# One stream of parts for all images, six product buffers, and delta*x made a third of the channels at a time

## The chip, the cores and the metric

The kernel runs on one core of one Trainium2 chip. Time is device microseconds of one execution of the whole program; of the kernel before, three runs are given and their median is used. One more execution was recorded by the profiler, and every duration below comes from it.

Five engines work side by side, each on its own queue of instructions in program order: PE (matrix products; PEld is its weight load), DVE (vector), ACT (scalar functions), POOL (a second vector engine) and SP, which here only issues DMAs. They wait for one another through semaphores.

## The reference

Eight images of 56 x 56 positions and 192 channels pass through four layers. Each adds to x a function of its group-normalised input:

```python
x = x + gated_toeplitz(_gn(x))      # layer 0: silu(p) * (toeplitz along w + along h of q*v), projected
x = x + window_attention(_gn(x))    # layer 1: 7x7 windows, shifted by 3, 6 heads
x = x + depthwise_conv3x3(_gn(x))   # layer 2
x = x + selective_scan_2d(_gn(x))   # layer 3
```

Layer 3 is most of the work. From 384 inner channels u (after a projection, a 3x3 depthwise convolution and silu) it runs four scans over the 3136 positions: by rows, by columns, and both backwards. Each channel has 16 states:

```python
delta = softplus(delta + delta_bias)
dA  = exp(delta * A)                       # per channel, state and position
dBu = delta * u * Bm
h[l] = dA[l] * h[l-1] + dBu[l]             # the scan
y[l] = sum over states of h[l] * Cm[l]  +  D * u[l]
```

The four y are added, layer-normalised over the channels, multiplied by silu(z), projected to 192 channels and added to x. All of it is float32.

## The kernel before, in words

Three stages come first, for all images: the products q*v, the Toeplitz products of layer 0, and constants. Then, per image, there are three kinds of work.

**The front** of an image, `front(b)`, is a Python generator over five parts: `gate` (rest of layer 0), `attention` (layer 1), `conv2` (layer 2), `inner` (projection, convolution and silu of layer 3, three times 128 channels) and `steps`. `steps` runs over 14 groups (o, j): two orders o of the positions (rows, columns) and seven chunks j of 448 positions. A group makes B and C (one product into a bank, L851; a copy, L853; stored to `bc_d`) and delta for the two scans of that order (products at L861, ACT at L866, Softplus at L870), and stores delta to `dl_d`. All parts of all fronts use the same memory, `slab`, one part at a time. Front 0 runs alone, before any scan.

**The scans** of an image run over 4 slots (the four directions) x 7 chunks of 448 positions x 3 thirds d of the channels x 8 pairs k of states: `chunks` lists (image, slot, chunk) for all images, 224 in all, and `pairs` lists (chunk i, d, k), 5376 in all. For each pair g:

- `inject` (L991, POOL): hs = du * bm, where du = delta * x of this third (`times_x`, L979, POOL) and bm is B, sent to all partitions. hs has 5 buffers; it is issued two pairs ahead, by `feed`.
- `decay` (L1006, ACT): dA = exp(delta * A), two instructions into one of two PSUM buffers `ps_a`, one pair ahead.
- `scan` (L1015, DVE), then `times_c` (L1021): hc = h * cm, on POOL for k in (1, 4, 6), otherwise on DVE. hc has 4 buffers. POOL's product is issued one pair later than the scan.
- `add_up` (L1036, PE): the product of hc with an identity adds the states up in a PSUM bank; it is issued two pairs after the scan and frees hc. After eight pairs `sums` adds the bank to `ysum` on DVE (L1046 in slot 0, with D * x; L1050 otherwise).

The loads for the scans are all issued on SP: bm and cm of the next chunk by `load_bc`, a pair at a time in the last third; delta of the next chunk by `load_delta` and three thirds of x by `load_xc` (tile xcd, 4 buffers) at d = 1, k = 0. The three products `times_x` for the next chunk stand at (d, k) = (1, 6), (1, 7) and (2, 0); du has 4 buffers. In slot 0 another load of x, for `sums`, is issued at k = 2 and used at k = 4.

**The finish** of an image, `finish(b, j)`, normalises and projects chunk j of `ysum` (L883 to L935); it runs beside the first seven chunks of the next image's scans, each of which overwrites `ysum` again.

The order of instructions is fixed while the program is built. A class `Parts` holds generators (clients), and a model of when each engine is free (`t`, with prices in us such as 1.1 for a pair's `add_up`). After each pair the loop calls `parts.step(limit)`: for each client it issues the next bit of work as long as the model says that it fits under a limit for ACT, PE ("E") and DVE. A client that has a PSUM bank holds it until its next turn. Where work has to be complete, the loop calls `step(anything)`, with no limit, until it is:

```python
if i % (4 * NCH) == 0 and d == 0 and k == 0 and b + 1 < B:
    fronts[b + 1] = parts.add(front(b + 1), "front")
...
if i + 1 in range(4 * NCH, len(chunks), 4 * NCH):
    while fronts[b + 1] in parts.clients:
        parts.step(anything)
```

So front b + 1 begins with the scans of image b and must be complete in the last chunk of image b, at d = 1, k = 0 (L1173 to L1175). The last image has no front beside it.

Of the kernel before, what the change touches and what calls it, by code (L numbers as in the profile page):

```python
# [15 lines left out]
F32 = mybir.dt.float32  # L16
# [11 lines left out]
CH = 448  # L28
NCH = L // CH
# [4 lines left out]
ND = DI // 128  # L34
NG = 2
# [46 lines left out]
def model(ctx: ExitStack, tc: tile.TileContext, a: dict, out: bass.AP):  # L82
    nc = tc.nc
    B = out.shape[0]
# [195 lines left out]
    with (  # L280
# [79 lines left out]


        meter, costs = Meter(tc.nc), {}


        st = wp.tile([CP, 2, NCH, 6], F32, name="gn_st")
# [466 lines left out]
        def steps(b):  # L832

            w_x, xc, rc, dl = carve(slab, 128, (2, ND, 128), (2, ND, CH), (2, CH), (2, ND, CH))
            nc.sync.dma_start(out=w_x, in_=a["w_x"])
            todo = [(o, j) for o in range(2) for j in range(NCH)]

            def load_x(n):
                o, j = todo[n]
                nc.sync.dma_start(out=xc[:, n % 2], in_=xc_d[o][b][:, :, j * CH : (j + 1) * CH])  # L840

            load_x(0)
            yield 0, 0, 8.0
            for n, (o, j) in enumerate(todo):
                tok = slice(j * CH, (j + 1) * CH)
                if n + 1 < len(todo):
                    load_x(n + 1)
                yield 0, 1
                p = bank()
                for d in range(ND):  # L850
                    nc.tensor.matmul(p[:, :CH], w_x[:, o, d, :], xc[:, n % 2, d, :], start=d == 0, stop=d == ND - 1)  # L851
                yield 1, 0
                nc.scalar.copy(rc[:, n % 2, :], p[:, :CH])  # L853
                nc.sync.dma_start(out=bc_d[o][b][:, tok], in_=rc[64:, n % 2, :])
                for d in range(ND):
                    yield 0, 2
                    held = []
                    for s in range(2):
                        row = slice(32 * s, 32 * s + R)
                        held.append(bank())  # L860
                        nc.tensor.matmul(  # L861
                            held[s][:, :CH], w_dt[row, o, d * 128 : (d + 1) * 128], rc[row, n % 2, :], start=True, stop=True
                        )
                    yield 2, 0
                    for s in range(2):
                        nc.scalar.activation(  # L866
                            dl[:, s, d, :], held[s][:, :CH], AF.Identity, bias=dt_b[:, 2 * o + s, d : d + 1]
                        )
                yield 0, 0
                nc.scalar.activation(dl, dl, AF.Softplus)  # L870
                usual_functions()
                for s in range(2):
                    nc.sync.dma_start(out=dl_d[2 * o + s][b][:, :, tok], in_=dl[:, s])
            yield 0, 0

        def front(b):
            yield from gate(b)
            yield from attention(b)
            yield from conv2(b)
            yield from inner(b)  # L880
            yield from steps(b)
# [83 lines left out]

        def load_xc(i, d):
            b, slot, j = chunks[i]
            t = sp.tile([128, CH], F32, name="xcd", bufs=4)
            nc.sync.dma_start(out=t, in_=xc_d[slot // 2][b][:, d, j * CH : (j + 1) * CH])
            return t  # L970

# [3 lines left out]
            nc.sync.dma_start(out=delta[:, :, 1 : CH + 1], in_=dl_d[slot][b][:, :, j * CH : (j + 1) * CH])  # L975

        def times_x(i, d):
            du = dus[i, d] = sp.tile([128, 1, CH], F32, name="du", bufs=4)
            nc.gpsimd.tensor_mul(du[:, 0, :], deltas[i][:, d, 1 : CH + 1], xcs.pop((i, d)))  # L979

        def tokens(i):
# [35 lines left out]
        def times_c(g):  # L1017
            i, d, k = pairs[g]
            h = hss[g] if on_pool(d, k) else das[g]
            hc = hcs[g] = sp.tile([128, NG, CH], F32, name="hc", bufs=4)  # L1020
            (nc.gpsimd if on_pool(d, k) else nc.vector).tensor_mul(hc, h[:, :, tokens(i)[0]], cms[i, k])  # L1021

        def keep_state(g):
# [29 lines left out]
        class Parts:  # L1053
# [8 lines left out]
            def run(self, engine, cost, *after):  # L1062
                self.t[engine] = max(self.t[engine], 0.0, *after) + cost
                return self.t[engine]
# [25 lines left out]
                entry.held, entry.needs, *load = got  # L1090
                entry.ready = at + sum(load)

            def step(self, limit):
                old = [e for e in self.clients if e.held]
                for entry in old + [e for e in self.clients if e not in old]:
                    while entry in self.clients:
                        if entry.held and entry not in old:
                            break
                        if entry.needs + sum(e.held for e in self.clients if e is not entry) > 2:
                            break  # L1100
                        if not self.fits(entry, limit):
                            entry.waits += 1
                            break
                        entry.waits = 0
                        if entry in old:
                            old.remove(entry)
                        self.resume(entry)
# [27 lines left out]
        with tc.manual_schedule():  # L1135
            for k in range(NP):
                load_bc(0, k)
            load_delta(0)
            for d in range(ND):
                xcs[0, d] = load_xc(0, d)  # L1140
                times_x(0, d)
            ahead, last = 2, len(pairs) - 1
            parts = Parts()
            run = parts.run
# [6 lines left out]

            def take(g):
                times_c(g)
                after = scanned[g], summed[g - 4] if g > 3 else 0.0
                taken[g] = run("P", 2.0, *after) if on_pool(*pairs[g][1:]) else run("D", 1.09, *after)

            def prepare(g):
# [4 lines left out]
                feed(g)  # L1162
            initial(0), initial(1)
            prepare(0)
            fronts = {}
            ending, anything = None, dict.fromkeys("ADE", 1e9)
            for g, (i, d, k) in enumerate(pairs):
                b, slot, j = chunks[i]
                if i % (4 * NCH) == 0 and d == 0 and k == 0 and b + 1 < B:
                    fronts[b + 1] = parts.add(front(b + 1), "front")  # L1170
                more = i + 1 < len(chunks)
                if more and d == 1 and k == 0:
                    if i + 1 in range(4 * NCH, len(chunks), 4 * NCH):  # L1173
                        while fronts[b + 1] in parts.clients:
                            parts.step(anything)  # L1175
                    load_delta(i + 1)
                    for e in range(ND):
                        xcs[i + 1, e] = load_xc(i + 1, e)
                if more and (d, k) in ((1, 6), (1, 7), (2, 0)):
                    times_x(i + 1, d + k - 7 if d == 1 else 2)  # L1180
                    run("P", 1.08)
                pi, pd, pk = pairs[g - 1]
                if g + ahead <= last:
                    feed(g + ahead)
                if g and on_pool(pd, pk):
                    take(g - 1)
                if g:
                    keep_state(g - 1)
                    run("A", 0.15, scanned[g - 1])
                if g < last:  # L1190
                    prepare(g + 1)
                if g + 2 <= last:
                    initial(g + 2)
                    run("A", 0.12, taken[g - 3] if g > 2 else 0.0)
                scan(g)
                scanned[g] = run("D", 2.02, set_[g], fed[g])
                if not on_pool(d, k):
                    take(g)
                if g and pd == ND - 1 and pi + 1 < len(chunks):
                    load_bc(pi + 1, pk)  # L1200
                done = (i, d - 1) if d else (i - 1, ND - 1)
                if k == 2 and g > NP and chunks[done[0]][1] == 0:
                    xds[done] = load_xc(*done)
                if slot == 0 and b > 0 and (d, k) == (1, 4):
                    while ending.at < 3:
                        parts.step(anything)
                if k == 4 and g > NP:
                    sums(*done)
                if slot == 0 and b > 0 and ((j, d, k) == (0, 0, 5) or j + 1 < NCH and (d, k) == (2, 4)):
                    while ending in parts.clients:  # L1210
                        parts.step(anything)
                    ending = parts.add(finish(b - 1, j + (d == 2)), "finish")

                n1 = max(parts.t["D"], fed[g + 1], set_[g + 1])
                n2 = n1 + (2.02 if on_pool(*pairs[min(g + 1, last)][1:]) else 3.11)
                parts.step({"A": max(n2, fed[g + 2]) - 0.7, "E": n1 + 5.0, "D": 0.2})
                if g >= 2:
                    add_up(g - 2)
                    summed[g - 2] = run("E", 1.1, taken[g - 2])
# [108 lines left out]
```

## Time and profile before

| | |
|---|---|
| three runs, us | 23,043.6, 23,055.5 (median), 23,061.3 |
| profiled execution: its own time, its span | 23,085.3, 23,083.3 |
| first scan; last product of `add_up` | 3,727; 22,879 |
| PE, DVE, ACT, POOL busy in the span | 80%, 72%, 54%, 70% |
| mean granted PE clock | 0.887 |
| time of one image's scans, images 0 to 7 | 2331, 2486, 2469, 2468, 2453, 2467, 2459, 2014 |

The span is from the first to the last instruction that the profiler saw. Busy PE time is modelled and overlaps, so a PE share of 80% is not a share of its peak. The image times run from an image's first scan to that of the next image. In the views of the profile, "x" is a count, and a row of waits names who waited, for whom, the time in total, how often, and the longest. A wait for several semaphores is put down to the one that came last.

### The profile page before, as it was taken

Reading aid. Unit: us, or ns where it says so; the run is one execution under the profiler, and the core shown is the slowest. Engines: PE = TensorE matmul, PEld = TensorE weight load, DVE = VectorE, ACT = ScalarE, POOL = GpSimd, SP = SyncE. Lnnn points to the kernel's source line nnn. Section 1 sums busy time; section 2 is a strip of 40 time slices with the busy share of each in tenths; the row PEclk is TensorE's granted clock in tenths of the full one; section 3 lists DMA queues with packets and bytes.
Section 4 is the critical chain, followed back from the end, with each engine's and each line's share of the span. In section 5 each row is a group of like instructions: output and inputs, shape, how many; then the busy total and the mean of one; then the engine's idle time right before and its main releaser. Section 6 shows DMA issues by size and latency. Waiting matters only on the chain. (4 is left out here: it accounts for less than half of the span.)

```text
span 23083.3 us, 201064 instructions
## 1 busy us (share of the span) xinstructions
PE 18554.5 (80%) x58660; PEld 9730.9 (42%) x58660; DVE 16579.4 (72%) x13156; ACT 12534.0 (54%) x31864; POOL 16157.3 (70%) x8500
## 2 busy tenths in 40 slices
PE   8866678888887878888888888887888798887666
PEld 4566334434443435343543444343434353333323
DVE  3211114997789768986899778976898689877996
ACT  3211225655666565756565566656664657565554
POOL 0000004987789768976898778877897689778997
PEclk9987778999899989998999889998999899988888
DMA  3488225445544455345544454345534553454332
GB/s 89 109 196 178 67 62 171 135 123 168 167 135 131 142 169 146 124 135 172 151 134 129 161 162 137 122 147 177 148 115 146 168 157 119 140 172 139 126 122 89
DMA packets 2536339, 3220.44 MB, mean 140 GB/s; under 512 B 1045261, under 2 KB 2488687, under 8 KB 2504272
## 3 DMA queue, kind: packets, MB, share of 16 engines
q1 hardware_dynamic: 2515010, 3091.32, 45.2%
q0 software_dynamic: 15520, 116.14, 1.3%
q8 instruction: 465, 7.62, 0.1%
q14 instruction: 640, 5.24, 0.1%
q10 hardware_dynamic: 4704, 0.12, 0.0%
HBM read 2631.56 MB, written 575.48 MB: 139 GB/s over the span
## 5 line engine op out<-in xcount | busy, mean ns | idle before, releaser
L991 POOL TENSOR_TENSOR hs<-du,bm 128x896 f32<-128x896 f32 x5376 | 11124.4, 2102 | 110.1 <-DVE ps_a L1015 90.2
L1036 PE MATMUL ps_y<-hc,ident_sb 128*128 128x448 f32 x21504 | 9913.8, 597 | 947.8 <-POOL hc L1021 846.4
L1015 DVE TENSOR_TENSOR_SCAN ps_a<-ps_a,hs 128x898 f32<-128x898 f32 x3360 | 6793.9, 2022 | 1048.5 <-ACT ps_a L1006 871.5
L1006 ACT ACTIVATE ps_a<-delta,A_logs_sb 128x449 f32<-128x449 f32 x10752 | 6859.4, 638 | 322.2 <-DVE hs L1015 35.9
L1036 PEld LDWEIGHTS ps_y<-hc,ident_sb 128*128 128x128 f32 x21504 | 4339.0, 210 | 5095.4 <-issue 3594.3
L1021 POOL TENSOR_TENSOR hc<-hs,cm 128x896 f32<-128x896 f32 x2016 | 4067.0, 2017 | 2757.2 <-DVE hs L1015 1574.0
L1015 DVE TENSOR_TENSOR_SCAN hs<-ps_a,hs 128x898 f32<-128x898 f32 x2016 | 4064.5, 2016 | 810.3 <-ACT ps_a L1006 779.3
L1021 DVE TENSOR_TENSOR hc<-ps_a,cm 128x896 f32<-128x896 f32 x3360 | 3668.9, 1092 | 1166.1 <-PE ps_y L1036 883.2
L1028 ACT COPY state<-ps_a 128x2 f32<-128x2 f32 x3359 | 528.6, 157 | 4109.0 <-DVE hc L1021 4106.4
L979 POOL TENSOR_TENSOR du<-delta,xcd 128x448 f32<-128x448 f32 x672 | 716.0, 1066 | 1266.1 <-DMA xcd<-xc 1266.1
L263 PE MATMUL ps_tz<-tzx,tm 112*112 112x112 f32 x4608 | 889.3, 369 | 463.5 <-issue 294.7
L802 PE MATMUL ps_f<-slab 128*128 128x448 f32 x2646 | 1096.9, 551 | 85.0 <-DMA slab<-dg_d 58.0
L277 POOL DMA_DIRECT2D o<-tzx x192 | 97.8, 513 | 1490.9 <-DVE tzx L269 1340.1
L263 PEld LDWEIGHTS ps_tz<-tzx,tm 112*112 112x112 f32 x4608 | 883.8, 199 | 469.2 <-issue 468.1
L269 DVE COPY tzx<-ps_tz 112x448 f32<-112x448 f32 x288 | 179.9, 625 | 1172.3 <-PE ps_tz L263 862.0
L996 ACT COPY hs<-state 128x2 f32<-128x2 f32 x4608 | 817.5, 177 | 2.7 <-POOL hc L1021 2.6
L76 PE MATMUL ps_f<-slab 96*96 96x448 f32 (+6 forms) x2306 | 745.3, 519 | 76.1 <-DMA slab<-x 37.4
L269 ACT COPY tzx<-ps_tz 112x448 f32<-112x448 f32 x288 | 153.2, 532 | 1198.1 <-PE ps_tz L263 1067.2
L632 PE MATMUL ps_f<-ident_sb,slab 98*98 98x98 f32 x1344 | 337.9, 322 | 576.3 <-ACT slab L625 576.3
L734 PE MATMUL ps_f<-slab 96*96 96x448 f32 x1764 | 728.9, 549 | 46.4 <-DVE slab L721 46.4
L802 PEld LDWEIGHTS ps_f<-slab 128*128 128x128 f32 x2646 | 509.4, 193 | 598.0 <-issue 528.7
L861 PE MATMUL ps_f<-slab,w_dt_sb 12*128 12x448 f32 x1176 | 507.5, 787 | 309.8 <-ACT slab L853 234.9
(215 smaller groups left out, 17788.8 us busy)
## 6 DMA issues: line engine op xcount, KB each, us to landing
bm<-bc SPq DMA_DIRECT2D x1792, 448.0 KB
cm<-bc SPq DMA_DIRECT2D x1792, 448.0 KB
xcd<-xc SPq DMA_DIRECT2D x840, 224.0 KB
dl<-slab SPq DMA_DIRECT2D x224, 672.0 KB
delta<-dl SPq DMA_DIRECT2D x224, 672.0 KB
tzx<-qv SPq DMA_DIRECT2D x192, 588.0 KB
o<-tzx POOLq DMA_DIRECT2D x192, 588.0 KB, 16.3
slab<-x SPq DMA_DIRECT2D x224, 336.0 KB
```

The lines of the kernel that those rows point to most:

```text
L76: return f(*args, **kw)
L263: nc.tensor.matmul(po[:, c, :], t[:, c2 + c, :], x[:, :, c1 + c2 + c], start=True, stop=True)
L734: nc.tensor.matmul(p[:CP, :CH], dg[:, k, t, :], xp[:, u, k, dy : dy + 8, dx : dx + W], start=t == 0, stop=t == 8,)
L802: nc.tensor.matmul(p[:, :CH], dg[:, t, :], xp[:, 8 * j + dy : 8 * j + dy + 8, dx : dx + W], start=t == 0, stop=t == 8,)
L979: nc.gpsimd.tensor_mul(du[:, 0, :], deltas[i][:, d, 1 : CH + 1], xcs.pop((i, d)))
L991: nc.gpsimd.tensor_mul(hs[:, :, tokens(i)[0]], dus[i, d].to_broadcast([128, NG, CH]), bms[i, k])
L996: nc.scalar.copy(hss[g][:, :, tokens(i)[1]], src)
L1006: nc.scalar.activation(dA[:, n, :], deltas[i][:, d, at : at + CH + 1], AF.Exp, scale=negA[:, slot, d, c : c + 1])
L1015: nc.vector.tensor_tensor_scan(h, dA, hs, 0.0, ALU.mult, ALU.add)
L1021: (nc.gpsimd if on_pool(d, k) else nc.vector).tensor_mul(hc, h[:, :, tokens(i)[0]], cms[i, k])
L1028: nc.scalar.copy(states[i][:, d, NG * k : NG * k + NG], h[:, :, tokens(i)[2]])
L1036: nc.tensor.matmul(yps[i, d][:, :CH], ident, hcs[g][:, n, :], start=k + n == 0, stop=k + n == NP + NG - 2)
```

## The change

Three things are done together.

1. **One stream of fronts.** A new front is added whenever the one before is complete, not at the first pair of an image. A set `made` records which (image, o, j) groups of `steps` have been issued. Before `load_delta(i + 1)` the loop asks only that the group that chunk i + 1 reads is in it. `step` gets an argument `only`: where a front or a finish is forced, the other client goes on only if it holds a bank.
2. **Buffers.** hc has 6 buffers instead of 4, and the model knows it (`summed[g - 6]`). xcd and du have 2 instead of 4, which is the same memory. The limit for PE is 8.0 us after the next scan's start instead of 5.0.
3. **x and delta * x by thirds.** x of the next third is loaded at k = 0 of each third and multiplied with delta at k = 3 (in the last third, for the first third of the next chunk). The total of both stays the same.

```diff
+        made = set()
...
                 for s in range(2):
                     nc.sync.dma_start(out=dl_d[2 * o + s][b][:, :, tok], in_=dl[:, s])
+                made.add((b, o, j))
...
-            t = sp.tile([128, CH], F32, name="xcd", bufs=4)
+            t = sp.tile([128, CH], F32, name="xcd", bufs=2)
...
-            du = dus[i, d] = sp.tile([128, 1, CH], F32, name="du", bufs=4)
+            du = dus[i, d] = sp.tile([128, 1, CH], F32, name="du", bufs=2)
...
-            hc = hcs[g] = sp.tile([128, NG, CH], F32, name="hc", bufs=4)
+            hc = hcs[g] = sp.tile([128, NG, CH], F32, name="hc", bufs=6)
...
-            def step(self, limit):
+            def step(self, limit, only=None):
                 old = [e for e in self.clients if e.held]
                 for entry in old + [e for e in self.clients if e not in old]:
+                    if only is not None and entry is not only and not entry.held:
+                        continue
...
-            for d in range(ND):
-                xcs[0, d] = load_xc(0, d)
-                times_x(0, d)
+            xcs[0, 0] = load_xc(0, 0)
+            times_x(0, 0)
...
-                after = scanned[g], summed[g - 4] if g > 3 else 0.0
+                after = scanned[g], summed[g - 6] if g > 5 else 0.0
...
-            fronts = {}
+            ahead_of, b_next = None, 1
...
-                if i % (4 * NCH) == 0 and d == 0 and k == 0 and b + 1 < B:
-                    fronts[b + 1] = parts.add(front(b + 1), "front")
+                if ahead_of not in parts.clients and b_next < B:
+                    ahead_of = parts.add(front(b_next), "front")
+                    b_next += 1
                 more = i + 1 < len(chunks)
                 if more and d == 1 and k == 0:
-                    if i + 1 in range(4 * NCH, len(chunks), 4 * NCH):
-                        while fronts[b + 1] in parts.clients:
-                            parts.step(anything)
+                    b1, slot1, j1 = chunks[i + 1]
+                    while (b1, slot1 // 2, j1) not in made:
+                        parts.step(anything, ahead_of)
                     load_delta(i + 1)
-                    for e in range(ND):
-                        xcs[i + 1, e] = load_xc(i + 1, e)
-                if more and (d, k) in ((1, 6), (1, 7), (2, 0)):
-                    times_x(i + 1, d + k - 7 if d == 1 else 2)
-                    run("P", 1.08)
+                if k in (0, 3) and (d + 1 < ND or more):
+                    at = (i, d + 1) if d + 1 < ND else (i + 1, 0)
+                    if k == 0:
+                        xcs[at] = load_xc(*at)
+                    else:
+                        times_x(*at)
+                        run("P", 1.08)
...
                     while ending.at < 3:
-                        parts.step(anything)
+                        parts.step(anything, ending)
...
                     while ending in parts.clients:
-                        parts.step(anything)
+                        parts.step(anything, ending)
...
-                parts.step({"A": max(n2, fed[g + 2]) - 0.7, "E": n1 + 5.0, "D": 0.2})
+                parts.step({"A": max(n2, fed[g + 2]) - 0.7, "E": n1 + 8.0, "D": 0.2})
```

## The prediction

> **What bounds the kernel now.** I read first the page's busy shares: no engine is above 80%, so no single engine sets the 23,083 us; the answer must differ by stage. So I cut the trace at the first scan of a chunk (a chunk is 24 pairs) and asked the view of busy time by windows for one middle image and for the last one. The columns are: stretch, length, then PE, PEld, DVE, ACT, POOL busy, granted clock, DMA share, GB/s.
>
> ```profile
> 11118.00:11660.00 542.00, 479.49 (x1828) 274.65 (x1826) 448.20 (x354) 318.27 (x775) 453.15 (x240) 0.95 0.54 150
> 11660.00:12421.00 761.00, 613.14 (x2133) 298.30 (x2132) 715.19 (x607) 527.62 (x1656) 704.70 (x362) 0.91 0.41 126
> 12611.00:13159.00 548.00, 458.46 (x1168) 227.27 (x1166) 404.55 (x267) 301.21 (x685) 419.15 (x216) 0.91 0.48 154
> 13159.00:13329.00 170.00, 140.80 (x332) 57.99 (x332) 131.72 (x84) 134.62 (x267) 142.41 (x74) 0.84 0.59 205
> 13329.00:13481.00 152.00, 114.84 (x213) 45.36 (x211) 65.67 (x43) 96.50 (x161) 65.32 (x34) 0.72 0.43 145
> ...
> 21415.00:22809.00 1394.00, 937.64 (x1921) 418.78 (x1920) 1306.39 (x841) 733.44 (x1920) 1394.00 (x719) 0.87 0.38 125
> ```
>
> The last row is the floor: 20 chunks of image 7 with no other work beside them, 1394/20 = 69.7 us a chunk, POOL busy all the time. The others are image 3: chunks 1 to 6 (gate and finish) 90.3 us each, 7 to 15 and most of 16 (attention) about 76, 19 to 24 (inner) 91.3, 25 and 26 (steps) 85.0. **Then one chunk, the last, takes 152 us**, in which POOL and DVE are busy only 65 and 66 us. The view of waits for that stretch, "engine line <- what it waited for: us, times, longest", tells why; beside it are the waits of chunks 19 to 24, and two rows of the whole run:
>
> ```profile
> POOL hc L1021 <- DVE hs L1015: 79.6, 1, 79.6
> DVE hs L1015 <- ACT ps_a L1006: 75.1, 1, 75.1
> ```
> ```profile
> ACT slab L811 <- PE ps_f L802: 84.1, 21, 5.2
> ...
> DVE hc L1021 <- PE ps_y L1036: 77.6, 52, 9.2
> ```
> ```profile
> DVE hc L1021 <- PE ps_y L1036: 883.2, 594, 9.2
> DVE hs L1015 <- ACT ps_a L1006: 779.3, 106, 81.0
> ...
> POOL hc L1021 <- PE ps_y L1036: 645.1, 226, 9.5
> ```
>
> One scan waits 75.1 us for a decay that stands in ACT's queue behind the whole rest of the next image's front: the loop at L1173 empties it at that place. Such a wait is at each of the seven image ends (56.3, 81.0, 75.1, 75.1, 75.1, 75.2, 74.8 in the timeline), **513 us in all**, two thirds of the 779 us of that row. The other visible loss is hc: a product waits for PE to free one of four buffers.
>
> [...] at 13,440 us the decay waits 75 us though its own inputs are there. [...] in the timeline 448-column matmul instructions start 0.375 us apart in a dense stretch and 0.75 us apart after an idle one (12,785 us). [...] in the trace xcd loads issued just behind bm and cm land after 4.3 to 7.8 us.
>
> **Part 1: the lump at the image end goes.** The new test asks only for the one (image, o, j) group of steps that the next chunk reads. In the order of instructions as built, the changed kernel has no place where more than one pair's share of front work stands between two scans at an image end: before, 21.8 us of PE work stood there in image 0 and 31.5 in images 3 and 6; after, 2.2 us at most. The front of image 4 then ends in chunk 0 of image 4 instead of before it, each next one some tenths of a chunk later, and the last one at chunk 1 of image 7. So the 513 us go, and their work is done beside scans instead. How much work? In the lump one group of steps follows the other every 15.7 us (13,376.30 to 13,392.04 us at L861), so 513/15.7 = 33 groups. What does a group cost beside scans? Chunks 25 and 26 hold 36 PE calls each, 9 a group, so 4 groups, and take 85.0 - 69.7 = 15.3 us over the floor: 3.8 us a group. 33 x 3.8 = 126 us. **Net -513 + 126 = -387 us.** What covers it is ACT's idle time: ACT is busy 733/20 = 36.7 us in a floor chunk and 134.6/2 = 67.3 us in chunks 25 and 26, so 7.7 us a group, 67 of 85 us at 4 groups. If that cover is gone (more groups in a chunk, or a finish part beside them) a group costs up to those 7.7 us. Bounds of this part: 33 x 7.7 = 254 us given back (-259) to 33 x 2 = 66 (-447). In the first chunks of images 3 to 7 the groups lie beside a finish part; those chunks took 104 us before, for gate, finish and a DMA wait for w_p, so I put nothing more there, within +-30 for them all.
>
> **Part 2: finish is forced alone** (`only`). Before, each forced step also pushed front work without a limit. The order shows the same density in chunks 1 to 6 in both kernels (38 and 41 to 42 us of front PE work a chunk, 16 and 19 pairs over 3 us), so nothing; -30 to +30.
>
> **Part 3: six hc buffers, PE limit 8 for 5.** At most the 883 + 645 us of waits; but they don't stand alone. In an inner burst a pair costs PE 4 instructions of ps_y and 6 of the convolution, 10 x 0.375 = 3.75 us, over the 2.9 us of a floor pair, so PE is the bound and a buffer only lets the others run ahead. How far ahead? The timeline at 12,876 us: ACT waits in L811 for the convolution's bank until 12,876.45, then makes the two decays of the next pair until 12,878.4; DVE's product waited 2.57 us for hc until 12,877.95 and the next scan starts at 12,878.96. Without the hc wait that scan could start at 12,878.4: 0.6 us gained of 2.57, since **ACT's in-order read of the same PE result is late next**. Gate (L477), conv2 (L743) and finish (L933) end in the same way on DVE. Low end: 0.6 us a burst, 4 bursts an image, 7 images: 17 us. High end: two more buffers hold 2 x 3.75 = 7.5 us a burst, x28 = 210, and all of the 35 us an image of chunks 1 to 6, x6 = 210, so 420. Below nothing: the wider PE limit puts front matmuls ahead of ps_y earlier; up to 50 lost. I take -60: most bursts end in such a read.
>
> **Part 4: x a third at a time.** 672 products stay 672 of 1.07 us on POOL; they move from three pairs in a row to one every eight. On the floor POOL is full either way: nothing. What is new is the lead: the load is issued at k = 0 and used at k = 3, on an SP queue that it shares with front stores, bm, cm and delta. In the trace the nearest case is x for `sums`, issued at k = 2 and used at k = 4: the tile view of xcd says
>
> ```profile
>   DVE ysum L1046: 29.3, 21
> ```
>
> 21 waits of 168, 29.3/168 = 0.17 us a load. Those over 0.3 us all stand at d = 2, just behind bm and cm loads, with one pair less of lead. In the new places only the 224 loads at d = 0 stand behind such loads: 224 x 0.17 = 39 us. A wait there stops POOL, and the feeds behind it, so a later scan, which has two pairs fed ahead: I count half, +20 us; low end 0, high end under the rivals. With two du buffers the product at k = 3 overwrites that of the third before, whose last feed was at k = 5 of its part, earlier on POOL's own queue: no wait.
>
> **Sum.** -387 - 60 + 20 = -427 us against the profiled execution's 23,085.3 gives 22,658. That execution stood 30 us (0.13%) over the median of the runs shown, 23,055.5, so **about 22,630 us**, 1.8% less.
>
> **Rivals.**
> 1. x loads become POOL's wait (the slower one). In image 7, where pairs are shortest, the seven waits of `sums` were 2.4 to 4.4 us, 3.2 on average. If the 224 loads at d = 0, which stand behind the last bm and cm loads, wait like that on POOL, it costs 224 x 3.2 = 717 us: 22,630 + 717 - 20, about 23,330. It decides from 427 + 20 = 447 us, that is 2.0 us for each of the 224. Against it: from the moment when SP may issue (POOL's product of pair 6 is done) POOL still has three feeds and one product to do, 3 x 2.1 + 2.0 = 8.3 us, and the loads landed after 4.3 to 7.8. For it: front stores on SP wait for ACT and hold the queue. 8%.
> 2. The hc buffers give all they can: -420 for -60, so 22,270. For it: 883 us of waits stand in the page; against it: the reads above. 18%.
> 3. The lump is only spread: a group of steps costs beside scans what it costs alone, or the test for `made` forces it all the same. Then -513 + 513 - 60 + 20 and about 23,020, no change or nearly. Against it: chunks 25 and 26 at 3.8 us a group, and the order as built. 7%.
>
> **How the numbers follow.** My forecast with its own bounds (22,480 to 22,830) gets 67%, the rivals 8, 18 and 7. What a measurement of this kernel can tell from no change is about 0.2%, 46 us. Faster by more: 67 + 18 + a part of rival 3 = 0.87; within: 0.05; slower: 0.08. The range reaches down into rival 2 (22,380) and up past the worst of part 1 (22,860).
>
> **What would show it.** In the changed profile: no DVE wait of 50 us or more at an image end, the last chunk of an image at 85 to 90 us instead of 152, and chunks 0 and 1 of image 7 longer by steps. The row DVE hc <- PE ps_y falls by more than the time does, and DVE <- ACT ps_a rises outside the image ends: right on part 3; both falling by hundreds: rival 2. A row POOL du <- DMA xcd of over 100 us beyond the 1266 us at the start: rival 1. Chunks with steps at 95 us or more: part 1's price was too low.

## The result, and the profile after

The changed kernel takes 22,802.3 us (median of 4 runs, 22,792.8 to 22,806.3) where the kernel before, on the same chip, takes 23,049.6 (4 runs). The ratio is 0.9894, 95% interval 0.9877 to 0.9911: 247 us less, where 427 were forecast. The profiled execution took 22,806.3 us (span 22,804.5), 279 less than that of before.

The view of busy time by windows, in stretches like those of before (image 3: chunks 1 to 6, 7 to 16, 19 to 24, 25 and 26, 27; then chunks 8 to 27 of image 7). The columns are stretch, length, PE, PEld, DVE, ACT, POOL busy, granted clock, DMA share, GB/s. The parts of the front now lie a chunk or so later than before.

```profile
11010.00:11549.00 539.00, 493.04 (x1898) 287.98 (x1897) 454.52 (x355) 312.88 (x736) 455.48 (x241) 0.94 0.57 158
11549.00:12311.00 762.00, 613.34 (x2155) 304.98 (x2154) 713.12 (x602) 532.37 (x1688) 704.16 (x362) 0.90 0.39 121
12500.00:13023.00 523.00, 459.37 (x1182) 225.67 (x1181) 413.22 (x282) 282.76 (x673) 422.36 (x217) 0.94 0.49 157
13023.00:13216.00 193.00, 155.00 (x366) 67.30 (x365) 133.74 (x85) 134.76 (x263) 142.24 (x73) 0.82 0.51 180
13216.00:13311.00 95.00, 77.74 (x182) 31.52 (x182) 66.96 (x43) 77.77 (x144) 74.78 (x39) 0.85 0.59 207
21202.00:22596.00 1394.00, 938.43 (x1920) 418.28 (x1919) 1310.68 (x839) 731.58 (x1916) 1393.90 (x719) 0.87 0.38 122
```

The floor is what it was, 1394 us for 20 chunks. The last chunk of the image is 95 us instead of 152. But chunks 25 and 26 take 193/2 = 96.5 us instead of 85.0. The view of waits from 3,900 to 22,600 us, where the other rows of before are answered (who waited, for whom, total, times, longest):

```profile
DVE ps_a L1017 <- ACT ps_a L1008: 1046.9, 523, 10.5
...
DVE hs L1017 <- ACT ps_a L1008: 401.3, 253, 9.7
...
POOL hc L1023 <- PE ps_y L1038: 156.7, 69, 5.3
```

And two rows of the page's costliest groups; behind the bar is the idle time before them:

```profile
L1023 DVE TENSOR_TENSOR hc<-ps_a,cm 128x896 f32<-128x896 f32 x3360 | 3668.7, 1092 | 271.1 <-PE ps_y L1038 34.9
...
L981 POOL TENSOR_TENSOR du<-delta,xcd 128x448 f32<-128x448 f32 x672 | 707.6, 1053 | 1401.1 <-DMA xcd<-xc 1397.7
```

The scan's longest wait for a decay is 10.5 us, where seven of 56 to 81 us stood. The waits of hc for PE fell from 883 + 645 us to 35 + 157. In their place the row DVE ps_a <- ACT ps_a doubled: in the same window it was 516.9 us before. Waits of that kind stand first in the new chunks with steps: in the last chunk of image 3 the longest row is

```profile
DVE ps_a L1017 <- ACT ps_a L1008: 20.2, 12, 3.4
```

Chunk times, as distances of first scans in the traces, show where the gain stopped. Image by image the scans differ from before by +9, -65, -48, -62, -50, -48, -32, +22 us, -274 together. The seven last chunks alone fell from 128, 155, 152, 152, 152, 153, 152 to 102, 95, 89, 95, 89, 88, 96: -390. **All other chunks together gave 116 us back.** Chunks 25 and 26 of images 0 to 6, where most of the steps lie, are 169 us longer than before; the rest is 53 us shorter.

### The profile page after: what moved, and what is told of

The parts are those of the page before. It is cut to its first block, busy times and chain, and to the rows that moved or that the text cites. A ratio compares the mean times of both kernels' runs of the same rounds, so it can differ in the third digit from the quotient of the medians.

```text
span 22804.5 us, 200303 instructions
## 1 busy us (share of the span) xinstructions
PE 18389.3 (81%) x58660; PEld 9684.3 (42%) x58660; DVE 16630.9 (73%) x13156; ACT 12477.6 (55%) x31864; POOL 16165.4 (71%) x8500
## 5 line engine op out<-in xcount | busy, mean ns | idle before, releaser
L998 ACT COPY hs<-state 128x2 f32<-128x2 f32 x4608 | 817.3, 177 | 0.0
L1030 ACT COPY state<-hs 128x2 f32<-128x2 f32 x2016 | 379.0, 188 | 567.1 <-DVE hs L1017 537.6
```

Source lines behind the costliest of these rows:

```text
L998: nc.scalar.copy(hss[g][:, :, tokens(i)[1]], src)
L1030: nc.scalar.copy(states[i][:, d, NG * k : NG * k + NG], h[:, :, tokens(i)[2]])
```

## The experiments

Each kernel was timed in 3 rounds beside the kernel before. Ratios are to that kernel, and differences of ratios are turned into us with 23,050.

| kernel | stream | hc | x by thirds | PE limit | us | before | ratio, 95% interval |
|---|---|---|---|---|---|---|---|
| the change | yes | 6 | yes | 8 | 22,802 | 23,050 | 0.9894 (0.9877 to 0.9911) |
| e1_stream | yes | 4 | no | 5 | 22,648 | 23,057 | 0.9822 (0.9807 to 0.9836) |
| e2_rest | no | 6 | yes | 8 | 23,152 | 23,057 | 1.0040 (1.0025 to 1.0055) |
| e3_limit5 | yes | 6 | yes | 5 | 22,656 | 23,057 | 0.9825 (0.9809 to 0.9842) |
| e4_hc4 | yes | 4 | yes | 8 | 22,757 | 23,057 | 0.9870 (0.9856 to 0.9885) |
| e8_stream_limit8 | yes | 4 | no | 8 | 22,823 | 23,044 | 0.9905 (0.9890 to 0.9919) |
| e10_hc4_limit5 | yes | 4 | yes | 5 | 22,614 | 23,044 | 0.9812 (0.9797 to 0.9826) |
| e9_x_early | yes | 4 | yes, earlier | 5 | 22,635 | 23,044 | 0.9823 (0.9808 to 0.9837) |
| e6_pe_price | yes | 6 | yes | 8, dearer PE | 22,910 | 23,044 | 0.9939 (0.9923 to 0.9956) |
| e11_steps5_rest8 | yes | 4 | yes | 5 in steps, else 8 | 22,767 | 23,101 | 0.9857 (0.9842 to 0.9872) |
| e12_steps8_rest5 | yes | 4 | yes | 8 in steps, else 5 | 22,783 | 23,101 | 0.9863 (0.9848 to 0.9878) |
| e13_hc6_plan4 | yes | 6, planned as 4 | yes | 5 | 22,689 | 23,101 | 0.9822 (0.9806 to 0.9839) |
| e15_limit5_5 | yes | 4 | yes | 5.5 | 22,588 | 23,045 | 0.9806 (0.9790 to 0.9822) |

### The parts alone

**e1_stream** does part 1 only: against the changed kernel everything but the stream is as before.

```diff
-            t = sp.tile([128, CH], F32, name="xcd", bufs=2)
+            t = sp.tile([128, CH], F32, name="xcd", bufs=4)
...
-            hc = hcs[g] = sp.tile([128, NG, CH], F32, name="hc", bufs=6)
+            hc = hcs[g] = sp.tile([128, NG, CH], F32, name="hc", bufs=4)
...
-                after = scanned[g], summed[g - 6] if g > 5 else 0.0
+                after = scanned[g], summed[g - 4] if g > 3 else 0.0
...
+                    for e in range(ND):
+                        xcs[i + 1, e] = load_xc(i + 1, e)
+                if more and (d, k) in ((1, 6), (1, 7), (2, 0)):
+                    times_x(i + 1, d + k - 7 if d == 1 else 2)
...
-                parts.step({"A": max(n2, fed[g + 2]) - 0.7, "E": n1 + 8.0, "D": 0.2})
+                parts.step({"A": max(n2, fed[g + 2]) - 0.7, "E": n1 + 5.0, "D": 0.2})
```

> The stream of fronts alone: made, only and the early start of the next front; hc stays at 4 buffers, xcd and du at 4 with three loads at once, PE limit 5. Theory A (a group of steps costs more in the changed kernel because limit 8 issues 4.3 to 4.7 groups a chunk, against 4.0 here and before): the group goes back to 3.8 us, the image ends bring -387 us, so about 22,660. Theory B (a group beside scans costs about 5.7 us at any density, since ACT is blocked in its queue by reads of PE results): -513 + 98 x 5.7 - 65 x 4.1 = about -220, so about 22,830. Theory C (thirds of x cost POOL waits): as A or B but without the 134 us of waits for xcd, so under 22,750 without any gain from hc.

Measured: -409 us. The stream alone brings more than the whole change. Its last chunks are 88, 86, 85, 81, 81, 110, 127 us, -385 together, and all its other chunks are 53 us shorter than before instead of 116 longer. The 110 and 127 us are remainders still forced, since in this kernel the fronts fall behind image by image.

**e2_rest** does everything but the stream: the loops of `fronts` as before, the rest as changed.

```diff
-                if ahead_of not in parts.clients and b_next < B:
-                    ahead_of = parts.add(front(b_next), "front")
-                    b_next += 1
+                if i % (4 * NCH) == 0 and d == 0 and k == 0 and b + 1 < B:
+                    fronts[b + 1] = parts.add(front(b + 1), "front")
```

> Everything but the stream: six hc buffers, PE limit 8, x and delta*x by thirds; fronts begin and are forced once an image as before. The lumps at the image ends stay. Theories A and B: inner chunks gain 50 to 60 us in all, the rest nothing, so 22,980 to 23,000 (a tighter packing of steps shortens the lump a little: down to 22,900). Theory C: the waits for xcd cost more than hc gains, so 23,050 to 23,120.

Measured: +95 us. The lump shrinks (the last chunks are 113 to 141 us), but chunks 25 and 26 now take 88 to 100, where they took 83 to 89. So buffers, limit and thirds together cost time, with the stream or without it.

**e3_limit5** and **e4_hc4** each take one thing out of the changed kernel: the limit, or the two buffers.

```diff
-                parts.step({"A": max(n2, fed[g + 2]) - 0.7, "E": n1 + 8.0, "D": 0.2})
+                parts.step({"A": max(n2, fed[g + 2]) - 0.7, "E": n1 + 5.0, "D": 0.2})
```

> The changed kernel with the PE limit back at 5.0. Steps are issued at 4.0 groups a chunk instead of 4.3 to 4.7, and the fronts end later, in chunk 2 of image 7. Theory A: the group costs 3.8 us again, 98 x 1.9 = 186 us less than the changed kernel at most, so 22,620 to 22,700. Theory B: the group costs the same, so 22,800 to 22,850.

```diff
-            hc = hcs[g] = sp.tile([128, NG, CH], F32, name="hc", bufs=6)
+            hc = hcs[g] = sp.tile([128, NG, CH], F32, name="hc", bufs=4)
...
-                after = scanned[g], summed[g - 6] if g > 5 else 0.0
+                after = scanned[g], summed[g - 4] if g > 3 else 0.0
```

> The changed kernel with hc and its model back at 4 buffers. If the six buffers are worth the 55 us that the inner chunks suggest, 22,850 to 22,870, with the hc waits on PE back at hundreds of us and the waits for ACT's decays lower by nearly as much. If they are worth all the 1300 us of waits that went, over 23,000. If they only let PE fall behind and make ACT wait (theory B in its strong form), under 22,790.

Measured: -400 us for limit 5.0, so the limit took (0.9894 - 0.9825) x 23,050 = 159 us; -300 for four buffers, which are thus no worse than six (0.9870 against 0.9894, intervals overlap).

**e8_stream_limit8** is e1_stream with 8.0 left in the last line of its diff, and **e10_hc4_limit5** is e4_hc4 with 5.0 there.

> The stream alone (four hc buffers, x as before) with the PE limit at 8.0. It differs from the stream alone in the limit only, and from the changed kernel with four hc buffers in the thirds of x only. If the limit is the loss by itself, 22,740 to 22,800 (100 to 150 us over the stream alone); if the loss needs the six buffers, within 40 us of the stream alone's 22,648.

> Stream and thirds of x, with four hc buffers and PE limit 5. It differs from the stream alone in the thirds only, and from the changed kernel with limit 5 in the hc buffers only. If POOL's waits for xcd (about 100 us in the page of each kernel with thirds) reach the end, 22,720 to 22,750, and then the six buffers are worth about as much in the kernel with limit 5; if they are covered, 22,640 to 22,660 and the six buffers are worth nothing.

Measured: the limit costs the stream alone (0.9905 - 0.9822) x 23,050 = 191 us. The stream with x by thirds (0.9812) beats the change; from e1's 0.9822 it is not told apart. Two chains of single edits now lead from before to the change, and each adds up to its -0.0106 (in us):

| | stream | then | then | then |
|---|---|---|---|---|
| by e8, e4 | -410 | limit 8: +191 | x by thirds: -81 | six hc: +55 |
| by e10, e13, e3 | -410 | x by thirds: -23 | six hc, then planned as six: +23, +7 | limit 8: +159 |

The first and the limit's terms stand far outside the intervals (0.0015 each, some 35 us). The -81 of x by thirds stands just outside them (0.9890 to 0.9919 against 0.9856 to 0.9885); the other terms are not told from zero.

### Why the buffers brought nothing

**e13_hc6_plan4** is e10_hc4_limit5 with six buffers, while the model goes on reckoning with four, so that the order of instructions stays the same (in the traces it is, instruction by instruction, on ACT, DVE, POOL and PE).

```diff
-            hc = hcs[g] = sp.tile([128, NG, CH], F32, name="hc", bufs=4)
+            hc = hcs[g] = sp.tile([128, NG, CH], F32, name="hc", bufs=6)
```

> Limit 5, thirds of x, six hc buffers, but the planner reckons with four: the order of the instructions is then that of the kernel with four buffers, and only the buffers differ. If two more buffers can only help: 22,550 to 22,614, and the 43 us between four and six buffers are due to the order that the planner makes for six. If they cost by themselves (DVE and POOL run ahead and collide with something else): 22,640 to 22,670. If the waits on PE go and the waits on ACT take their place exactly: within 20 us of 22,614.

Measured: 0.9822 against 0.9812, no gain. The view of waits, 3,900 to 22,600 us, of e10 with four buffers:

```profile
DVE hc L1023 <- PE ps_y L1038: 845.8, 607, 10.8
...
POOL hc L1023 <- PE ps_y L1038: 612.6, 264, 9.9
...
DVE ps_a L1017 <- ACT ps_a L1008: 544.2, 330, 4.9
...
DVE hs L1017 <- ACT ps_a L1008: 283.6, 100, 27.4
```

and of e13 with six:

```profile
DVE ps_a L1017 <- ACT ps_a L1008: 932.2, 461, 7.1
...
DVE hs L1017 <- ACT ps_a L1008: 524.4, 243, 28.9
```

The waits for PE are down from 846 and 613 us to 8 and 87, and 932.2 + 524.4 - 544.2 - 283.6 = 629 us of waits for decays have come. Behind which instruction the decays stand is shown by ACT's read of the convolution in the groups by line, of e10 and then of e13:

```profile
L812 ACT ACTIVATE slab<-ps_f,cb_sb 128x448 f32<-128x448 f32 x147 | 93.2, 634 | 590.2 <-PE ps_f L803 590.2
```
```profile
L812 ACT ACTIVATE slab<-ps_f,cb_sb 128x448 f32<-128x448 f32 x147 | 93.3, 635 | 774.7 <-PE ps_f L803 774.7
```

ACT waits 184 us more for the same products of PE: with hc free, the scans arrive early at a decay that stands behind that read. Followed back along ACT's queue to the last instruction that itself had to wait, the scans' waits that end behind this read are 50 us in e10 and 436 in e13. That is the larger part of the 629; most of the rest (27 to 217 us) stands behind decays that wait for a scan to free `ps_a`.

### Where the limit costs

In the order of instructions as built, limit 5.0 issues one group of steps in six pairs, limit 8.0 one in six and one in five by turns: 4.0 groups a chunk against 4.3 to 4.7. In between stand ACT's Softplus (2.45 us a group, L871) and two table loads of 1.28 us (L871 and L321). **e12_steps8_rest5** sets 8.0 while a front is in its steps and 5.0 elsewhere, **e11_steps5_rest8** the reverse; both are otherwise e10_hc4_limit5.

```diff
+            part[0] = "steps"
...
+            part[0] = ""
...
-                parts.step({"A": max(n2, fed[g + 2]) - 0.7, "E": n1 + 8.0, "D": 0.2})
+                parts.step({"A": max(n2, fed[g + 2]) - 0.7, "E": n1 + (8.0 if part[0] else 5.0), "D": 0.2})
```

> The reverse: PE limit 8.0 in steps, 5.0 otherwise, so 4.6 to 4.7 groups a chunk in steps alone. Theory A1: 22,720 to 22,760, as with limit 8 everywhere and four hc buffers (22,757). Theory A3: about 22,650, since the other parts are most of the front.

> Stream, thirds of x, four hc buffers; the PE limit is 5.0 while a front is in its part steps and 8.0 otherwise. Theory A1 (limit 8 costs through the density of steps groups, whose ACT work leaves no room for the decays): 22,560 to 22,640, as with limit 5 everywhere or a little better since no group is forced at the last image ends. Theory A3 (limit 8 costs in every part, since front products stand ahead of ps_y): 22,680 to 22,740.

Measured: 0.9863 and 0.9857 against 0.9812: the limit costs in both places, 118 and 104 us, and in both at once (e4) 134. The parts do not add up.

In the steps the price can be read. Some chunks of a run have steps beside the scans and nothing else: no other part of a front, no finish, no forced work. The table takes all of these, with the groups counted by ACT's reads of delta's products (L867, six a group), and the floor of 69.7 us. Its first two rows differ in the limit for the steps alone, and its last two in the limit alone.

| | such chunks | us each | over the floor | groups each | us a group |
|---|---|---|---|---|---|
| e10, limit 5 | 9 | 84.1 | 14.4 | 4.0 | 3.6 |
| e12, limit 8 in steps | 20 | 94.6 | 24.9 | 4.4 | 5.6 |
| e3, limit 5, six hc | 9 | 86.7 | 17.0 | 4.0 | 4.2 |
| the change, limit 8, six hc | 12 | 93.5 | 23.8 | 4.5 | 5.3 |

For the 98 groups of e12 this makes 98 x (5.6 - 3.6) = 196 us, an estimate; some 56 us of forced remainders that e10 has and e12 has not go off it, which leaves about 140 where 118 were measured. More groups in a chunk and other places for their instructions come together in these kernels, so which of the two makes a group dearer is not told.

Chunks 25 and 26 of image 0 show it closer. e10 has 8 groups in them, the change and e12 have 9. The windows of e10:

```profile
5768.00:5852.00 84.00, 72.37 (x168) 29.54 (x168) 66.25 (x43) 70.98 (x140) 72.90 (x38) 0.84 0.60 197
5852.00:5934.00 82.00, 71.16 (x169) 29.45 (x168) 65.80 (x43) 69.84 (x137) 70.28 (x36) 0.88 0.63 214
```

of the change:

```profile
5772.00:5866.00 94.00, 76.91 (x176) 30.62 (x174) 67.45 (x44) 76.58 (x142) 74.43 (x38) 0.82 0.60 199
5866.00:5962.00 96.00, 80.97 (x186) 32.50 (x186) 67.18 (x43) 77.73 (x144) 74.67 (x39) 0.82 0.60 206
```

and of e12:

```profile
5775.00:5872.00 97.00, 84.97 (x182) 33.82 (x180) 66.48 (x42) 77.41 (x144) 73.30 (x39) 0.79 0.57 187
5872.00:5972.00 100.00, 87.41 (x172) 33.60 (x172) 66.47 (x42) 72.32 (x140) 67.82 (x35) 0.71 0.56 188
```

The waits in those two chunks, of e10:

```profile
DVE ps_a L1017 <- ACT ps_a L1008: 16.8, 7, 3.3
...
ACT slab L867 <- PE ps_f L862: 9.9, 7, 2.7
...
DVE hs L1017 <- ACT ps_a L1008: 8.9, 3, 3.4
...
DVE hc L1023 <- PE ps_y L1038: 5.1, 4, 1.9
```

of the change:

```profile
DVE ps_a L1017 <- ACT ps_a L1008: 34.2, 19, 3.4
...
ACT slab L867 <- PE ps_f L862: 17.4, 19, 1.9
DVE hs L1017 <- ACT ps_a L1008: 10.9, 7, 3.4
...
ACT slab L867 <- DMA dl<-slab: 6.2, 10, 1.0
```

and of e12, in which the lines of the scans stand two lower:

```profile
DVE ps_a L1019 <- ACT ps_a L1010: 29.0, 15, 4.3
...
ACT slab L867 <- PE ps_f L862: 23.1, 18, 3.0
DVE hc L1025 <- PE ps_y L1040: 23.1, 14, 2.1
```

The change's two chunks take 190 - 166 = 24 us more than e10's, and its scans wait longer for ACT by about as much: 51.5 us against 29.0, with the rows that name another instruction of ACT, hs L998, left out above (3.3 and 6.4 us). But the change also has six hc buffers. e12 has four as e10 has, and takes 31 us more: 18 of them are DVE's longer waits for PE to free hc (23.1 us against 5.1), and about 10 its scans' longer waits for ACT. So with four buffers the looser limit costs in the steps by both waits, and in the change nearly all of it comes by ACT. The groups by line show ACT's side for the whole run. ACT's read of delta's products, of e10, of e12 and of the change (L867 is the same line in all):

```profile
L867 ACT ACTIVATE slab<-ps_f,dt_b_sb 128x448 f32<-128x448 f32 x588 | 340.4, 626 | 113.1 <-PE ps_f L862 102.7 <-DMA dl<-slab 9.7
```
```profile
L867 ACT ACTIVATE slab<-ps_f,dt_b_sb 128x448 f32<-128x448 f32 x588 | 350.1, 629 | 272.8 <-PE ps_f L862 185.0 <-DMA dl<-slab 85.8
```
```profile
L867 ACT ACTIVATE slab<-ps_f,dt_b_sb 128x448 f32<-128x448 f32 x588 | 348.7, 629 | 250.1 <-PE ps_f L862 195.2 <-DMA dl<-slab 54.7
```

With limit 5.0 in the steps ACT stands idle 113 us (119 in e11) ahead of this instruction, with 8.0 250 to 273: the products of PE come late (185 and 195 us of it, where e10 has 103), and `dl` is still being stored from the group before (86 and 55 us, where e10 has 10). ACT's decays stand behind it in its queue. Between e3 and the change, which differ in the limit alone, the idle time there goes from 127 to 250 us.

With four buffers the waits of hc for PE grow too, wherever the looser limit is. DVE's and POOL's together, from 3,900 to 22,600 us, are 1458 us in e10 (845.8 and 612.6), 1772 in e12, 1695 in e11 and 1954 in e4. So this mark does not tell the places apart, and what the 104 us outside the steps consist of is not shown. Six buffers take these waits away, but not the cost: beside six buffers the limit takes 159 us (e3 against the change).

### A theory that was not decided, and x

**e6_pe_price** asked whether the limit costs because the model's prices for PE are too low. It is the changed kernel with PE priced as the trace of before has it: in a dense stretch its 448-column instructions start 0.375 us apart, so the two of a product make 0.75 us and the four of a pair's `add_up` 1.5.

```diff
-    TIMES = {"tensor": ("E", 0.04, 1.25e-3), "scalar": ("A", 0.2, 0.83e-3),
+    TIMES = {"tensor": ("E", 0.0, 1.68e-3), "scalar": ("A", 0.2, 0.83e-3),
...
-                    summed[g - 2] = run("E", 1.1, taken[g - 2])
+                    summed[g - 2] = run("E", 1.5, taken[g - 2])
```

> The changed kernel, limit 8 and six buffers, with the planner's prices for PE as measured: a 448-column product 0.75 us instead of 0.60, a pair's add_up 1.5 instead of 1.1. Theory A2: the loss at limit 8 comes from a planner that believes PE to be done earlier than it is, so that ACT and DVE read PE's results too early in their queues and block the decays; then the DVE waits for ACT's decays fall by hundreds of us and the time to 22,600 to 22,700. Theory A1: only the number of steps groups in a chunk counts; they stay at 4.0 to 4.3 here, so also about 22,650, but the inner chunks stay as they are in the changed kernel (94 a pair of chunks) and the DVE waits for ACT too. Against both: front work that is issued later ends up forced at the image ends, lumps of 20 to 40 us in several images.

Measured: slower than the change. The chunks with front work are cheaper (image 0, inner and steps: 71 to 91 us), but the front is no longer done in time, and the last chunks of images 1 to 6 take 248 to 254 us. Since the lump is back, the run does not decide whether the prices were a part of the limit's cost. The view of waits shows it:

```profile
DVE hs L1017 <- ACT ps_a L1008: 950.1, 186, 137.4
```

**e9_x_early** is e10_hc4_limit5 with x loaded seven pairs ahead of its use instead of three, into three buffers, so that POOL does not wait for it.

```diff
-            t = sp.tile([128, CH], F32, name="xcd", bufs=2)
+            t = sp.tile([128, CH], F32, name="xcd", bufs=3)
...
+                if k == 4 and (d + 2 < ND or more):
+                    at = (i, d + 2) if d + 2 < ND else (i + 1, d + 2 - ND)
+                    xcs[at] = load_xc(*at)
```

> As the one before, but x has three buffers and is loaded at k = 4 of the third before, seven pairs ahead of its product instead of three. The waits POOL du <- DMA xcd go from about 100 us to under 20. If those waits cost what they last, this is 80 to 100 us faster than with three pairs of lead; if POOL's wait is covered by the two pairs fed ahead, within 30 us.

Measured: no gain (0.9823 against 0.9812). Its whole run has the one wait at the start and no other in this row:

```profile
POOL du L981 <- DMA xcd<-xc: 1263.2, 1, 1263.2
```

So the 110 us of such waits in e10, and the 134 in the change, are covered.

### A limit between

**e15_limit5_5** has 5.5 in e10_hc4_limit5.

> The stream with x by thirds and four product buffers, with the PE limit at 5.5 instead of 5.0. In the order of instructions as built a chunk with steps still issues 4.0 groups, but the front of the next image is no longer so far behind at the ends of images 5 and 6, where limit 5.0 still forced a remainder (last chunks of 108 to 127 us). Theory that the limit costs only through more groups of steps in a chunk and denser inner chunks: the forced remainders go, 25 to 50 us gained on limit 5.0, a ratio of 0.979 to 0.981 to the kernel before. Rival, that any looser limit costs in proportion (175 us for 3.0, so 29 for 0.5): 0.982 to 0.984.

Measured: 0.9806, the fastest of all; it does not stand apart from e10's 0.9812, but the forced remainders are gone (last chunks 82 to 87 us in all seven images, where e10 had 108 and 118 in images 5 and 6). It beats the change by (0.9894 - 0.9806) x 23,050 = 203 us.

## Why the prediction was right, and where it was not

**What bounds the kernel: right.** The lump at the image end was the wait to take away, and the floor did not move.

**The whole.** 22,802 us lies inside the stated 22,480 to 22,830, but only 28 us from its upper end: the direction and the main term held, and the gain fell short by 180 us.

**Part 1: right for the stream, wrong for the change.** Forecast -387; e1_stream gave -409. That they are so close is partly luck: e1's last chunks of images 5 and 6 still hold some 69 us of forced work that the forecast had gone, and its other chunks became 53 us shorter, though groups of the lump moved into them; why is not known. In the change the term that failed is "33 x 3.8 = 126". The 3.8 us is the price at 4 groups a chunk, and e10 has 3.6 there. But the changed order issues 4.3 to 4.8 groups in such a chunk, for all 98 groups and not only the 33, and there a group cost 5.3 us. The prediction named this case ("if that cover is gone (more groups in a chunk ...)") with 7.7 us at most, and took the other value; it gives no count of groups a chunk for the changed order.

**Part 2: consistent.** Chunks 1 to 6 of image 3 are 539 us against 542. It was not tried alone.

**Part 3: the reasoning held, both sizes failed.** The waits of hc fell by 1336 us where the time fell by 279, and ACT's read of the same product is late next, as forecast (L812, 590 us in e10 and 775 in e13). But of the -60 nothing came: six buffers measure +23 to +55 us, not resolved from zero. The line "up to 50 lost" for the wider limit is the larger error: it costs 159 us beside six buffers, 191 alone. This is the loss that part 1 shows as a dearer group, together with what the limit costs outside the steps, and not a second one. The reason given, ps_y standing behind front matmuls, fits what four buffers show (hc's waits for PE, 1458 us in e10 and 1954 in e4). It left out that ACT's reads of PE's products come later too, and beside six buffers that stays (ACT is idle 127 us ahead of L867 in e3 and 250 in the change).

**Part 4: the sign was wrong beside limit 8.0.** Forecast +20; the thirds gain 81 us there, and 23, not told from zero, beside 5.0. The waits of POOL for x came (134 us where 39 were worked out) and cost nothing (e9). Why spreading the products gains was not tried.

**The sum.** Forecast -387 - 60 + 20 = -427. Measured by the second chain: -410 + 30 - 23 + 159 = -244. In this account part 3 with its limit is off by 249 us; parts 1 and 4 came out 66 us better than forecast and hid as much of it.

**Rivals.** 1 is out: POOL's waits for x passed the mark of 100 us set for it and nothing became slower, so the mark was badly chosen. 2 is out: waits for decays took the place of hc's. 3 is out: a group beside scans costs 3.6 to 5.6 us in the kernels of the table, not 15.7.

**Marks.** No scan waits 50 us at an image end; last chunks are 88 to 102 us where 85 to 90 were named; chunks 0 and 1 of image 7 grew from 83 and 79 to 94 and 89. "Chunks with steps at 95 us or more: part 1's price was too low" is the one that decided: those with steps alone took 88 to 99, 93.5 in the mean, and about half of them reached the mark. Before they took 83 to 86.

**Open.** Why the limit's costs in the steps and outside do not add up, and what those outside consist of. Whether the number of groups in a chunk or their places make a group dearer. Whether six buffers cost something beside limit 8.0. Why x by thirds gains beside limit 8.0. Six buffers with x as before were not tried; in the change their memory is what the thirds free.

## What to carry to other kernels

When a lump is spread beside other work, count in the order as built how dense it becomes and look where it lands, since its price there need not be the old price: here 3.6 us a group at 4.0 groups a chunk and 5.6 at 4.4. A wait for a buffer that repeats need not be worth what it lasts: here some 1360 us of such waits went for nothing, mostly because another engine's queue had a read of PE's products next (from e10 to e13 ACT's wait at L812 rose from 590 to 775 us). So the repeating waits showed the missing buffers here (with six, DVE's 846 us and POOL's 613 fell to 8 and 87), but not the time (0.9812 became 0.9822). Change a planner's limit in a run of its own; it decided more here than the buffers it came with.

## What was not expected of the hardware

Among the kernels with the stream the mean granted PE clock goes with the limit: 0.897 to 0.899 in the profiled runs of e1, e3, e10, e9 and e15 (limit 5.0 or 5.5), 0.895 in e13, and 0.890 to 0.893 in those of the change, e4, e6, e8, e11 and e12. The two kernels with the old lump are lower, 0.887 before and 0.883 in e2. In the two chunks shown it is 0.84 and 0.88 in e10, 0.82 and 0.82 in the change, 0.79 and 0.71 in e12. The clock is not the whole of the loss: at 0.84 the first of e10's two chunks takes 84 us with 4 groups, and at 0.85 the change's last chunk of image 3 takes 95 us with 4.7 (28 reads at L867). Whether it is a part of the cost, these runs don't tell.
